# Turning the sorted rows of an MoE stage: blockwise loads and the vector engine in place of TensorE and ACT

## The chip, the cores and the metric

The kernel runs on one core of one Trainium2 chip. The time is the device time of one execution in microseconds (us); lower is better. The engines of a core work side by side, each from its own queue, in order: PE (TensorE: matrix products; its weight loads are listed apart as PEld), DVE (VectorE), ACT (ScalarE), POOL (GpSimd) and SP (SyncE, which here only issues DMAs). Between engines order is kept by semaphores.

## The reference

One transformer block with modulation (adaLN): attention, and behind it a mixture of experts (MoE). The change touches the MoE alone. Cut to that part, it computes:

```python
x = x + ga * attention(h)                       # 2 x 1024 tokens, dim 256, 16 heads
h = _layernorm(x) * (1 + cb) + sb
xf = h.reshape(-1, 256)                         # 2048 tokens
logits = xf @ router_w.T                        # 8 experts
topk_vals, topk_idx = jax.lax.top_k(logits, 2)
topk_w = jax.nn.softmax(topk_vals)
order = jnp.argsort(topk_idx.reshape(-1))       # the 4096 pairs, sorted by expert
x_sorted = xf[order // 2]
y1 = ragged_dot(x_sorted, w1 of each expert)    # 256 -> 2 * 176
gate, up = jnp.split(y1, 2, axis=-1)
y2 = ragged_dot(silu(gate) * up, w2 of each expert)   # 176 -> 256
y = (y2[inv] * topk_w).reshape(T, 2, 256).sum(axis=1)
x = x + gb * y
```

All numbers are float32.

## The kernel before, in words

**Attention, to about 1148 us.** Four blocks of 512 tokens go through 16 heads each. While they run, the tokens of finished blocks are normalised, routed and scattered by POOL's indirect DMAs into `sorted_x`, a DRAM tensor of 39 tiles (`ALL`) of 128 rows in the order of the experts. Each expert's rows are padded to whole tiles. A row has 260 numbers (`ROW`): the token's 256, and four behind them (its weight, its batch, the row of `results` that it goes to). The first 17 tiles (`FULL`) are filled by the first 12 tiles of 128 tokens; the others need the second set of scatters as well, that of the last block's tokens, which runs inside the MoE stage. The weights `w1` (`load_w1`, L355) and `w2` are loaded in the last attention block.

**The MoE stage, from about 1148 us.** Each sorted tile m goes through these steps:

- `Sorted(m)`, L1587: one DMA on SP's queue loads 128 rows of 260 numbers into `x`, one row a partition. It runs up to 7 tiles (`PRE`) ahead, into 2 + 5 buffers of their own and then a ring of 18.
- `turn` (L1594, L1596): the matmul needs the 256 features on the partitions. Two TensorE transposes of 128x128 write `xp` into PSUM, ACT copies it to `xT`.
- `up` (L1603 to L1613): four matmul instructions `su` with the expert's `w1`, ACT's Silu `sg`, DVE's product `sact`.
- `gates` (L1656): DVE makes the output gate of the tile's rows.
- `turn_back` (L1619, L1621): two TensorE transposes `ap`, and ACT's copy `sactT`.
- `down` (L1628 to L1639): four matmul instructions `sy` with `w2`; DVE scales them into `ysb`; POOL scatters the 128 rows to `results` by an indirect DMA.

At the end the rows of `results` are read back (`y`), added in pairs with `xs`, and written out.

The loop over m gives turn of tile m, up of m−1, turn_back of m−3 (m−2 from `LATER` = 24 on) and down of m−4 (m−3 from then on) in one round:

```python
tiles[m].turn()
tiles[m - 1].up()
sooner = m >= LATER
while back < min(m - 2 + sooner, ALL):
    tiles[back].gates()
    tiles[back].turn_back()
    back += 1
while done < min(m - 3 + sooner, ALL):
    tiles[done].down()
    done += 1
```

This order of the source is not quite the order in which an engine meets the instructions: when the program is built, the framework places them in each engine's queue by its own estimate of when their operands are there. On the chip a queue is then fixed, and served in order.

Of the kernel before, what the change touches and what calls it, by code (L numbers as in the profile page):

```python
# [43 lines left out]
FP = mybir.dt.float32  # L44
# [6 lines left out]
P = 128  # L51
# [9 lines left out]
def tile_adaln_attention_moe(  # L61
# [15 lines left out]
    nc = tc.nc  # L77
    B, N, D = x.shape
    DC = D // P
    T = B * N  # L80
    NT = T // P
# [13 lines left out]
    TOP = 2  # L95
    SETS = ((0, (NBLK - 1) * QT), ((NBLK - 1) * QT, NT))


    FULL = -((E * (P - 1) - TOP * SETS[0][1] * P) // P)
# [55 lines left out]
    ident = const.tile([P, P], FP, name="ident")  # L155
# [9 lines left out]
    SIDE = 32  # L165
# [45 lines left out]
    sorted_x = dram.tile([ALL * P, ROW], FP, name="sorted_x")  # L211
    results = dram.tile([(TOP * NT + ALL) * P, D], FP, name="results")

    class Scattered:
# [3 lines left out]
        def __init__(self, name):  # L218
            self.name, self.all = name, []
# [21 lines left out]
    into_x = Scattered("into_x")  # L241
# [5 lines left out]
    with ExitStack() as attn:  # L247
# [100 lines left out]
        w1_at = []  # L348

        def load_w1():  # L350
            w1_in = w1.rearrange("(c p) e i -> p c e i", p=P)
            pieces = []
            for c in range(DC):
                piece = keep.tile([P, E, I2], FP, tag="w1" + "ab"[c], name=f"w1_{c}")
                nc.sync.dma_start(out=piece, in_=w1_in[:, c])  # L355
                pieces.append(piece)
            w1_at.append(pieces)

# [624 lines left out]
        class Settle:  # L983
# [43 lines left out]
            def turn(self, i):  # L1027


                t = self.blk * QT + i  # L1030
                b = t // TPB
                row = rows[:, t, :D]
                mean, rs = self.of_x[i]
                nc.vector.scalar_tensor_tensor(
                    row, xs[:, t, :], mean, one_cb[:, b, :], ALU.subtract, ALU.mult
                )
                nc.vector.scalar_tensor_tensor(row, row, rs, sb[:, b, :], ALU.mult, ALU.add)
                self.rT[i] = self.wide.tile([P, DC, P], FP, tag="h", name=f"rT_{t}")
                if self.blk < NBLK - 1:
                    turned(row, self.rT[i], f"r{t}")  # L1040
                    return
                tp = self.psum.tile([P, DC, P], FP, tag=self.tag, name=f"tp2_{t}")
                for c in range(DC):
                    nc.tensor.transpose(tp[:, c, :], row[:, ts(c, P)], ident)
                nc.scalar.copy(self.rT[i], tp)
# [388 lines left out]
        for blk in range(NBLK):  # L1434
# [11 lines left out]
            for h in range(HEADS):  # L1446
                src = q if h < HEADS - HG else after
# [50 lines left out]
            if blk == NBLK - 1:  # L1498
                at(1, 6, load_wout_again)
                at(11, 0, load_w1)  # L1500
                at(QT + 2, 4, place_first, work)
                slots = [(k, t) for k in range(TOP) for t in range(0, SETS[0][1], 3)]
                for n, (k, t) in enumerate(slots):
                    if k and not t:
                        at(QT + 3 + n, 2, choose_second, *SETS[0])
                    at(QT + 3 + n, 3, on_vector, scatter_some, k, t, 3)
                at(HEADS - HG + 1, 0, load_w2)

            for i, h in enumerate(((6, 8, 11, 13), (7, 9, 11, 13))[blk] if blk < 2 else ()):
                t = TPB + blk * QT + i  # L1510
# [23 lines left out]
    with ExitStack() as moe:  # L1534
# [3 lines left out]
        mg = moe.enter_context(tc.tile_pool(name="mg", bufs=3))  # L1538
# [4 lines left out]
        ps_t = moe.enter_context(tc.tile_pool(name="ps_t", bufs=3, space=PSUM))  # L1543
# [11 lines left out]
        def row_buffer(name):  # L1555


            return mr.tile([P, TOP * D], FP, tag="x", name=name)
# [4 lines left out]
        def expert(m):  # L1563
# [10 lines left out]
                loaded.update(zip(range(m, m1), values))  # L1574
            return loaded[m]

        class Sorted:


            def __init__(self, m):  # L1580
                self.m = m
                if m < EARLY + NEXT:
                    pool = mx if m < EARLY else me
                    self.x = pool.tile([P, ROW], FP, name=f"x_{m}")
                else:
                    self.x = row_buffer(f"x_{m}")[:, :ROW]
                load = nc.sync.dma_start(out=self.x, in_=sorted_x[ts(m, P), :])  # L1587
                into_x.read(load, TOP * (SETS[0][1] if m < FULL else NT))

            def turn(self):  # L1590
                m = self.m
                tp = ps_t.tile([P, DC, P], FP, tag="t", name=f"xp_{m}")
                for c in range(DC):
                    nc.tensor.transpose(tp[:, c, :], self.x[:, ts(c, P)], ident)  # L1594
                self.xT = mg.tile([P, DC, P], FP, tag="xT", name=f"xT_{m}")
                nc.scalar.copy(self.xT, tp)  # L1596

            def up(self):
                m = self.m
# [99 lines left out]
        for m in range(ALL + 3):  # L1699
# [17 lines left out]
            if SCATTERS <= m < SCATTERS + TOP:  # L1717
                k = m - SCATTERS
# [18 lines left out]
        for i in range(BESIDE):  # L1737
            m = ALL - 4 + i // 2
# [59 lines left out]
```

## Time and profile before

| what | value |
|---|---|
| time, median of 3 runs | 1266.76 us (1266.58 to 1268.63) |
| the profiled execution: its time | 1273.54 us |
| the profiled execution: its span, first to last instruction | 1271.8 us |
| granted TensorE clock, mean | 0.995 |
| instructions | 13505 |
| DMA | 79.26 MB in 87975 packets, mean 62 GB/s |

The profile comes from one execution, taken by the hardware profiler. Every engine has a row of busy time; "the chain that ended last" is followed back from the last instruction, at each step to what released it or to the instruction before it on its engine. A group of instructions is given as line, engine, operation, output<-inputs with shapes and count, then its busy time and the mean ns of one, then the idle time of the engine in front of it and what ended that. A span has the length between the first and the last instruction, so it is a little below the time. Matmuls are pipelined and their ends are modelled: where matmuls follow closely, the distance of their starts is the better measure.

The MoE stage takes about 124 of the 1271.8 us. Its 78 xp transposes (L1594) and 39 copies (L1596) are the instructions that the change replaces, for 31 of the 39 tiles.

### The profile page before, as it was taken

To read this page: it belongs to the slowest core of one execution; us is meant where nothing else is said; L and a number is where in the kernel's file an instruction comes from. 1 tells how busy PE (TensorE), PEld (TensorE's weight loads), DVE (VectorE), ACT (ScalarE), POOL (GpSimd) and SP (SyncE) were. 2 spreads that over 40 slices of the span, in tenths; PEclk is the share of its full clock that TensorE was granted. 3 is DMA by queue.
4 is the path that set the end of the run, shared out by engine and by line. 5 is a ranking of instruction groups with operands and counts; after the bars stand their busy time and mean duration, and the time that the engine had idled before them with its cause. 6 is when DMAs were issued, how large, how long until landed. Compare 5 with 4: busy or idle time off the path is not lost.

```text
span 1271.8 us, 13505 instructions
## 1 busy us (share of the span) xinstructions
PE 1244.7 (98%) x4134; PEld 686.0 (54%) x4134; DVE 848.5 (67%) x1763; ACT 452.7 (36%) x884; POOL 187.3 (15%) x223
## 2 busy tenths in 40 slices
PE   8999999999999999999999999999999999999895
PEld 5544444448545454548545454557545444477573
DVE  7577777666866876666866666666758675547355
ACT  3533333331333343431333434321333344314331
POOL 3210301010100201010000000000000223204542
PEclk9999999999999999999999999999999999999998
DMA  7011020211011111111011061012011242113426
GB/s 265 0 34 34 6 83 15 73 35 42 13 44 44 40 48 43 49 38 35 12 51 38 34 198 34 34 54 76 13 56 32 68 141 92 34 34 97 134 84 236
DMA packets 87975, 79.26 MB, mean 62 GB/s; under 512 B 43520, under 2 KB 66688, under 8 KB 87648
## 3 DMA queue, kind: packets, MB, share of 16 engines
q1 hardware_dynamic: 82624, 67.06, 17.3%
q0 software_dynamic: 3408, 9.38, 2.0%
q10 hardware_dynamic: 1872, 1.97, 0.4%
q8 instruction: 34, 0.56, 0.2%
q14 instruction: 37, 0.30, 0.1%
HBM read 58.29 MB, written 20.08 MB: 62 GB/s over the span
## 4 chain that ended last, share of the span: by engine, by line
PE 90%; DVE 3%; POOL 2%; issue 2%; DMA 1%; another core or an unknown queue 0%; ACT 0%; SPq 0%; POOLq 0%; DVEq 0%; ACTq 0%
PE s L767 34%; PE o L782 33%; PE q L693 7%; PE pr L925 6%; PE pr L846 2%; PE su L1603 2%; PE sy L1628 1%; POOL results L1639 1%; PE kv L466 1%; PE q L642 1%; PE ap L1619 0%; PE xp L1594 0%; PE lg L1051 0%; DMA wide_q<-row_q 0%; DVE h L404 0%
## 5 line engine op out<-in xcount | busy, mean ns | idle before, releaser
L767 PE MATMUL s<-qT,kT 128*128 128x512 f32 x1024 | 524.4, 595 | 0.7 <-ACT qT L1310 0.7
L782 PE MATMUL o<-p,vs 128*128 128x512 f32 x1024 | 521.6, 592 | 0.0
L771 ACT ACTIVATE p<-s 128x512 f32<-128x512 f32 x512 | 304.8, 597 | 511.3 <-PE s L767 498.1
L787 DVE TENSOR_TENSOR sum<-sum,p 128x512 f32<-128x512 f32 x384 | 264.2, 688 | 178.8 <-ACT p L771 175.9
L782 PEld LDWEIGHTS o<-p,vs 128*128 128x128 f32 x1024 | 194.3, 190 | 243.5 <-issue 238.7
L767 PEld LDWEIGHTS s<-qT,kT 128*128 128x128 f32 x1024 | 191.5, 190 | 186.4 <-issue 177.2
L742 POOL TENSOR_TENSOR rn_q<-rn_q,minus_half 128x16 f32<-128x16 f32 x15 | 44.1, 2940 | 319.0 <-DVE rn_q L738 300.4
L787 DVE TENSOR_TENSOR sum<-p,p 128x512 f32<-128x512 f32 x64 | 43.9, 685 | 38.5 <-ACT p L771 38.5
L1603 PE MATMUL su<-w,xT 128*128 x156 | 54.2, 471 | 3.6 <-ACT xT L1596 3.5
L551 DVE STREAM_TRANSPOSE turned_q<-sq_q 128x512 f32<-128x512 f32 x60 | 42.4, 707 | 18.2 <-ACT sq_q L655 18.2
L925 PE MATMUL pr<-wout_sb,qT 128*128 128x128 f32 x384 | 50.0, 276 | 0.0
L583 DVE TENSOR_TENSOR qT<-qT,wide_q 128x512 f32<-128x512 f32 x60 | 41.1, 686 | 10.7 <-DMA wide_q<-row_q 10.7
L583 DVE TENSOR_TENSOR qT<-qT,wide 128x512 f32<-128x512 f32 x64 | 43.5, 679 | 6.9 <-DMA wide<-row 6.8
L1639 POOL DMA_INDIRECT results<-ysb,x x39 | 40.4, 1037 | 50.5 <-DVE ysb L1636 39.2
L655 ACT ACTIVATE sq_q<-qT 128x512 f32<-128x512 f32 x56 | 35.2, 629 | 34.6 <-DVE qT L700 26.9
L551 DVE STREAM_TRANSPOSE turned<-sum 128x512 f32<-128x512 f32 x64 | 45.5, 710 | 1.8
L925 PEld LDWEIGHTS pr<-wout_sb,qT 128*128 128x128 f32 x384 | 46.2, 192 | 0.1
L693 PE MATMUL q<-rows,wq_sb 128*128 128x256 f32 x168 | 45.4, 379 | 0.0
L789 ACT COPY qT<-o 128x512 f32<-128x512 f32 x64 | 37.4, 584 | 19.7 <-PE o L782 19.6
L552 DVE TENSOR_REDUCE parts<-turned 128x16 f32<-128x512 f32 x64 | 43.3, 676 | 1.1
L1628 PE MATMUL sy<-w2s,sactT 128*128 x156 | 40.3, 383 | 1.5 <-issue 1.3
L552 DVE TENSOR_REDUCE parts_q<-turned_q 128x16 f32<-128x512 f32 x60 | 40.8, 680 | 0.7
(330 smaller groups left out, 1067.9 us busy)
## 6 DMA issues: line engine op xcount, KB each, us to landing
wide<-row SPq DMA_DIRECT2D x64, 256.0 KB
wide_q<-row_q SPq DMA_DIRECT2D x60, 256.0 KB
sorted_x<-zero SPq DMA_DIRECT2D x1, 5070.0 KB
x<-sorted_x SPq DMA_DIRECT2D x39, 130.0 KB
y<-results SPq DMA_DIRECT2D x14, 256.0 KB
w<-in_w_dram SPq DMA_DIRECT2D x2, 1408.0 KB
wout_sb<-in_wout_dram SPq DMA_DIRECT2D x1, 2048.0 KB
wq_sb<-in_wq_dram SPq DMA_DIRECT2D x1, 1536.0 KB
```

The lines of the kernel that those rows point to most:

```text
L551: nc.vector.transpose(turned.rearrange("p c k -> p (c k)"), src)
L552: latest["vector"] = nc.vector.tensor_reduce(parts[:, i, :], turned, AX.X, ALU.add).ins
L583: nc.vector.tensor_tensor(q.head(h), q.head(h), wide, ALU.mult)
L693: nc.tensor.matmul(ps[:, k, :].rearrange("p (t k) -> p t k", k=P), x, y, start=True, stop=True,)
L767: latest["tensor"] = nc.tensor.matmul(s, kT[:, ts(b * NJ + j, P)], q.head(h), start=True, stop=True).ins
L771: nc.scalar.activation(p, s, AF.Exp)
L782: latest["tensor"] = nc.tensor.matmul(outs[h], vs[:, b * NJ + j, :], p, start=(j == 0), stop=(j == NJ - 1)).ins
L787: latest["vector"] = nc.vector.tensor_tensor(sums[h], first, p, ALU.add).ins
L925: nc.tensor.matmul(ps[:, piece, :], halves(g)[:, pair, head, t, i, :], w[:, g * HG // TWO + pair, :], start=False, stop=(g == NG - 1 and m ...
L1603: nc.tensor.matmul(u, self.xT[:, c, :], w1_flat[c][:, bass.ds(at, I2)], start=(c == 0), stop=(c == DC - 1),)
L1628: nc.tensor.matmul(y, self.actT[:, c, :], w2_flat[:, c * D :][:, bass.ds(at, D)], start=(c == 0), stop=(c == 1),)
L1639: ins = nc.gpsimd.indirect_dma_start(out=results, out_offset=bass.IndirectOffsetOnAxis(ap=self.x[:, TO : TO + 1].bitcast(I32), axis=0), in ...
```

## The change

A tile's features are no longer put on the partitions by TensorE for tiles 8 to 38. DVE has a block transpose: it turns each block of 32 partitions by 32 numbers, but moves no block to other partitions. So the loads move the blocks. A tile's row index is (a, i) with four groups a of 32; its 256 features are split into four groups of 64. Load b of four brings, for all 128 rows, the 64 features of group b, to the 32 partitions of group b, with row group a as the first free index; each run is 256 bytes. Then partition group b holds only features of group b, and DVE's one block transpose of 128 x (4 x 2 x 32) puts feature j of a block on partition j of the group, and the row on the free axis. The fifth load brings the four numbers behind the features.

With that, the feature on partition p = (b, j) of half c is 64 b + 32 c + j, where it was 128 c + p. So `w1` is loaded in the same permuted order, in four pieces of 32 partitions for each half, for all tiles. Tiles 0 to 7 (`FIRST_TILES`) are still turned on TensorE and copied by ACT; their loads permute the features within each row (two DMAs with runs of 128 bytes, and one for the four numbers behind them).

Counted, 62 transposes with their weight loads and 31 ACT copies are gone; 31 DVE transposes of 128x256 are new; SP issues 179 loads of `x` where there were 39, and 8 of `w1` where there were 2.

```diff
         def load_w1():
-            w1_in = w1.rearrange("(c p) e i -> p c e i", p=P)
+            w1_in = w1.rearrange("(b c j) e i -> c b j e i", c=DC, j=SIDE)
             pieces = []
             for c in range(DC):
                 piece = keep.tile([P, E, I2], FP, tag="w1" + "ab"[c], name=f"w1_{c}")
-                nc.sync.dma_start(out=piece, in_=w1_in[:, c])
+                for b in range(P // SIDE):
+                    nc.sync.dma_start(out=piece[ts(b, SIDE)], in_=w1_in[c, b])
                 pieces.append(piece)
...
+        FIRST_TILES = 8
+        in_blocks = sorted_x.rearrange("(m a i) d -> m i a d", a=P // SIDE, i=SIDE)
+
         class Sorted:
...
-                load = nc.sync.dma_start(out=self.x, in_=sorted_x[ts(m, P), :])
-                into_x.read(load, TOP * (SETS[0][1] if m < FULL else NT))
+                n = D // (P // SIDE)
+                parts = [(self.x[:, D:], sorted_x[ts(m, P), D:])]
+                if m < FIRST_TILES:
+                    src = sorted_x[ts(m, P), :D].rearrange("p (b c j) -> c p b j", c=DC, j=SIDE)
+                    for c in range(DC):
+                        parts.append((self.x[:, ts(c, P)].rearrange("p (b j) -> p b j", j=SIDE), src[c]))
+                else:
+                    for b in range(P // SIDE):
+                        to = self.x[ts(b, SIDE), :D].rearrange("i (a k) -> i a k", k=n)
+                        parts.append((to, in_blocks[m][:, :, ts(b, n)]))
+                for to, src in parts:
+                    with nc.allow_non_contiguous_dma(reason="some numbers of each row"):
+                        load = nc.sync.dma_start(out=to, in_=src)
+                    into_x.read(load, TOP * (SETS[0][1] if m < FULL else NT))
 
             def turn(self):
-                m = self.m
-                tp = ps_t.tile([P, DC, P], FP, tag="t", name=f"xp_{m}")
-                for c in range(DC):
-                    nc.tensor.transpose(tp[:, c, :], self.x[:, ts(c, P)], ident)
-                self.xT = mg.tile([P, DC, P], FP, tag="xT", name=f"xT_{m}")
-                nc.scalar.copy(self.xT, tp)
+                self.xT = mg.tile([P, DC, P], FP, tag="xT", name=f"xT_{self.m}")
+                if self.m < FIRST_TILES:
+                    tp = ps_t.tile([P, DC, P], FP, tag="t", name=f"xp_{self.m}")
+                    for c in range(DC):
+                        nc.tensor.transpose(tp[:, c, :], self.x[:, ts(c, P)], ident)
+                    nc.scalar.copy(self.xT, tp)
+                    return
+                nc.vector.transpose(
+                    self.xT.rearrange("p c (a i) -> p a c i", i=SIDE),
+                    self.x[:, :D].rearrange("p (a c j) -> p a c j", c=DC, j=SIDE),
+                )
```

## The prediction

> **What bounds the kernel now.** I read the page first: busy shares, clock row, and the shares of the chain that ended last.
>
> ```profile
> PE 1244.7 (98%) x4134; PEld 686.0 (54%) x4134; DVE 848.5 (67%) x1763; ACT 452.7 (36%) x884; POOL 187.3 (15%) x223
> ...
> PEclk9999999999999999999999999999999999999998
> ...
> PE 90%; DVE 3%; POOL 2%; issue 2%; DMA 1%; another core or an unknown queue 0%; ACT 0%; SPq 0%; POOLq 0%; DVEq 0%; ACTq 0%
> ```
>
> TensorE is the bound over the whole program, at full clock. But the change lives in the last tenth, the stage of the 39 sorted tiles, so next I read the chain in order of time there.
>
> ```profile
> 1203.96 1.19 PE su L1603 x4
> 1205.36 0.86 PE sy L1628 x4
> 1206.45 1.19 PE su L1603 x4
> ```
>
> One tile lasts 1206.45 − 1203.96 = 2.49 us (2.488 by the raw starts): su 1.19, two ap transposes 0.22, sy 0.87, and two xp transposes 0.22 in the hole ahead of the next su. PE has no gap. It has none because it works on four tiles at once: between su of tile k and su of tile k+1 it does ap of k−2, sy of k−3 and xp of k+2, so every result has a tile's time or more to come back through ACT and DVE. The groups of the stage give the costs:
>
> ```profile
> L1594 PE MATMUL xp<-ident,x 128*128 128x128 f32 x78 | 15.0, 274 | 0.3 <-ACT proj L869 0.3
> L1596 ACT COPY xT<-xp 128x256 f32<-128x256 f32 x39 | 14.6, 375 | 31.2 <-PE xp L1594 24.7 <-remote 3.8 <-PE su L1603 1.9
> L1636 DVE SCALAR_TENSOR_TENSOR ysb<-sy,x,gate 128x256 f32<-128x256 f32 x32 | 15.4, 482 | 14.6 <-PE sy L1628 9.2 <-remote 3.6 <-PE xp L1594 1.5
> ```
>
> ACT and DVE idle in front of these because they wait for PE. Last, the timeline of the last tile, where nothing is left to overlap with it. It is the one place in this profile that shows what a tile costs alone:
>
> ```profile
> 1251.94 1.35 PE L1603 MATMUL su<-w,xT 128*128 x4
> ...
> 1253.32 0.32 ACT L1611 ACTIVATE sg<-su 128x176 f32<-128x176 f32 x1 [1.62 <-PE su L1603]
> ...
> 1253.67 0.34 DVE L1613 TENSOR_TENSOR sact<-sg,su 128x176 f32<-128x176 f32 x1
> ...
> 1254.06 0.29 PEld L1619 LDWEIGHTS ap<-ident,sact 128*128 128x128 f32 x2
> ...
> 1254.68 0.37 ACT L1621 COPY sactT<-ap 128x256 f32<-128x256 f32 x1 [0.71 <-PE ap L1619]
> ...
> 1255.31 0.73 PEld L1628 LDWEIGHTS sy<-w2s,sactT 128*128 128x128 f32 x4 [0.27 <-ACT sactT L1621]
> ```
>
> From the first su matmul to the first possible ap transpose pass 1254.20 − 1251.94 = 2.27 us; from that transpose to sactT's end 1255.05 − 1254.20 = 0.85 us.
>
> **The change part by part.** The basis is the profiled execution: span 1271.8, time 1273.54. It is 6.8 us above the median of 1266.76. Three tiles from 1178.7 to 1193.8 take 15.1 us instead of 7.5 there (first stretch under the rivals), about that difference. I apply differences to the median.
>
> *Removed from PE.* 31 tiles × 2 transposes. The group's 274 ns is a modelled length: the two start 0.109 us apart and move su by 0.217 us. Where PE is the bound, that is 0.217 us a tile, 31 × 0.217 = 6.7 us at most. The Trainium skill (VectorE: DVE Perf Modes, The three transpose paths) prices a TensorE transpose of 128x128 at 390 ns, which would make it 62 × 0.39 = 24 us. The raw starts decide: 6.7.
>
> *Removed from ACT.* 31 copies of 0.375: off the path, since ACT waits for PE.
>
> *Added to DVE.* 31 block transposes of 128x256. The nearest row has the same shape:
>
> ```profile
> L437 DVE STREAM_TRANSPOSE blocks_r<-rows 128x256 f32<-128x256 f32 x12 | 5.3, 441 | 0.0
> ```
>
> I take 0.44. DVE has 0.48 + 0.34 + 0.48 = 1.30 us a tile; 1.74 is under any period below. Price on the path 0, and 0.44 a tile if DVE were late.
>
> *Loads.* Tiles 0 to 7 take 3 DMAs instead of 1, tiles 8 to 38 take 5, all on SP's queue: 179 issues instead of 39. Back to back the old loads are issued 0.474 us apart, and landed in 2.1 to 3.1 us, with eight in flight at most. Five cost 2.37 us a tile. Tiles 8 to 16 have all their issues by 1148 + (18 + 45) × 0.474 = 1178, ahead of their use. Tiles 17 and later may only start after the second set of scatters, at 1186.2: 22 × 2.37 = 52 us, until 1238, some 2.4 us a tile. Tile 2 lands about 0.5 us late at the start (three issues from 1148.1 and a landing of 2.5 make 1151.6; its xp ran at 1151.27). I charge 0.5. How the 256-byte runs that change partitions issue and land is not shown. The nearest row is a load of 32 partitions in 128-byte runs (ns shortest, median, longest):
>
> ```profile
> L455 SPq DMA_DIRECT2D rT<-turned_r x96: 302/430/792, 342.0 to 957.3; - x96
> ```
>
> Its median is that of the x loads back to back (0.43), it landed in 1.5 to 1.8 us, its longest is 0.79. So the bounds are 0.474 an issue and 0.84 (0.79 and the 0.045 between two), 2.4 to 4.2 us a tile. I take 0.474, by the median.
>
> *w1.* 8 DMAs instead of 2 between 1037 and 1058 us, some ninety us ahead of use, beside attention's matmuls: 0. Without that cover, 6 × 0.47 = 2.8 us.
>
> *Moved: the order on PE.* This decides. Nothing in the source reorders up, turn_back and down, but the order of an engine's queue is fixed when the program is built, by the framework's own estimate of when operands will be there, and the changed program has another. Listed by tile:
>
> ```
> before  xp[k+1] su[k] ap[k-2] sy[k-3]                          (1 tile later from 35 on)
> after   su[13] ap[11] sy[10] | su[15] ap[14] sy[13] ap[15] sy[14]
>         su[17] sy[16] ap[17] | su[18] sy[17] ap[18] | su[19] sy[18] ap[19]
>         su[20] sy[19] ap[20] sy[20] | su[21] sy[20] ap[21] sy[21]
>         su[22] ap[22] sy[22] | su[23] ap[23] sy[23] | ... | su[38] ap[38] sy[38]
> ```
>
> From tile 22 on, PE does a whole tile before it starts the next: seventeen times what the old program does once, at its end. ap[k] waits at the head of PE's queue for DVE's sact[k], and behind it su[k+1], whose xT is long there, waits too. The Trainium skill (TensorE: Matmul & The Clock Gate, Part 2, Step-by-step) says that matmuls stay in program order, and only weight loads are pulled ahead. The trace has no matmul overtaking another. If they could overtake, the 6.7 us would stand; as they can't, each tile costs its latency.
>
> Period of a serial tile: 2.27 (su to ap) + 0.85 (ap, copy) + 0.05 (wait to weight load) + 0.97 (0.10 from sy's weight load to its matmul, 0.87 for sy until the next su starts) = 4.13 us. Taken with the lag that the last sy showed behind its predecessor (0.27 instead of 0.05) it is 4.35.
>
> - Tiles 8 to about 14: 9 × 0.217 = −1.95 (xp of 8 to 16); but by tile 15 PE has done one ap and sy pair (0.22 + 0.87) more: −0.9.
> - su[15] to su[22]: now 1211.26 − 1193.84 = 17.4. Afterwards 3.4 for tile 15; 2.5 for each of 16 to 19, because ap[k] follows 2.27 us behind su[k] with 0.22 of its own; 3.7 and 4.1 for 20 and 21: 21.1, +3.7.
> - su[22] to su[38]: now 1251.94 − 1211.26 = 40.7. Afterwards 16 × 4.13 = 66.1: +25.4 (by 4.35: +28.9).
> - The end: tile 38 takes as long as now, but the two earlier tiles' scatters no longer queue on POOL ahead of its own (issued at 1255.48, 1256.74, 1258.01; alone it could go at about 1256.7): −1.3.
> - The start: +0.5.
>
> Sum: −0.9 + 3.7 + 25.4 − 1.3 + 0.5 = +27.4. So 1266.8 + 27.4 = 1294 us; a profiled execution like the one shown would be 1301.
>
> The loads are hidden here: with 4.13 us a tile SP's 2.4 is no bound. POOL (1.08 a scatter) and ACT (0.69 a tile) are not either.
>
> **The rivals.**
>
> *Faster.* PE stays packed and each of 31 tiles saves 0.217: 1266.8 − 6.7 = 1260. For it: PE is the bound, DVE has room. Against it: it needs PE to start su[k+1] while ap[k] waits. To break even, the serial tiles would have to run in 4.13 − 27.4/16 = 2.4 us, but su to ap alone is 2.27 of that. Chance 0.04.
>
> *The loads bound it.* If an issue or landing is above 0.83 us (4.13 / 5), SP is slower than the serial chain: at 1.0 us an issue tiles 17 to 38 take 22 × 5 = 110, load 38 is issued at 1186 + 110 = 1296 in the trace's time and lands at 1298.5, against su[38] at 1251.9 + 28.7 = 1281 there: 18 more, 1312. For it: short runs, partition changed; eight in flight with 4 us landings would do half of that. Against it: the median of the row above, and DMA engines that are busy 0.32 of the stretch from 1211 to 1252 (shown next). Chance 0.05. Were the PE order the old one, the loads at 0.474 would give 2.37 to 2.42 a tile, 1265 to 1269: no change; 0.02.
>
> *The clock falls.* In the serial tiles PE works 2.27 of 4.13 us, in bursts with gaps up to about 1.1 us. Stretches of the stage, with busy time and instructions of PE, its weight loads, DVE, ACT and POOL, then clock, DMA share and GB/s:
>
> ```profile
> 1178.70:1193.84 15.14, 10.15 (x38) 6.63 (x37) 4.09 (x11) 3.36 (x11) 8.87 (x9) 0.89 0.55 174
> 1193.84:1211.26 17.42, 17.42 (x86) 13.04 (x85) 9.15 (x22) 7.14 (x21) 7.56 (x7) 1.00 0.38 106
> 1211.26:1251.94 40.68, 40.68 (x199) 30.63 (x198) 19.72 (x47) 16.59 (x49) 17.53 (x17) 1.00 0.32 106
> 1251.94:1261.00 9.06, 4.51 (x21) 3.11 (x19) 6.62 (x20) 1.02 (x3) 3.96 (x5) 1.00 0.90 330
> ```
>
> In the first, PE idled 2.8 us and the clock then was 0.5 for 3.4 us, an su taking 2.71 instead of 1.19; in the last, with PE busy half the time, it stayed 1.00. The skill's rule (TensorE: Matmul & The Clock Gate, The two states) puts a cold clock behind an idle window of about 3.4 us, which these gaps don't fill. At half clock PE's 2.27 doubles: up to 6.4 a tile, +36 more, 1330. In part of the stage only: 1305 to 1315. Chance 0.08.
>
> *Not what it says.* That the transposes don't go can be left out: the instructions of the changed program are 16 xp and 8 copies, for tiles 0 to 7.
>
> **How the numbers follow.** Serial tiles 0.81: 1294, by itself 1287 to 1302 (period 3.9 to 4.35 gives −4 to +4, the loads' start and the stretch around tile 15 ±3). Clock 0.08, loads 0.05, no change 0.02, faster 0.04. For the range I take in the lower end of the serial case and the near parts of the clock and load cases: 1285 to 1305. 0.2% is 2.5 us, about what a measurement of this kernel can tell from no change. Faster 0.04, same 0.02, slower 0.94.
>
> **What would show it.** In the trace after, su starts 4.1 us apart from tile 22 on; in its groups, ap idle behind DVE sact, about 1 us a tile, and sy behind ACT sactT, about 0.7; xp in 16 matmuls and copies xT 8; a DVE transpose at 0.44 x31; clock row unchanged; PE's share down to about 97%. Wrong, if su starts come 2.3 to 2.5 apart in the last 16 tiles (order not binding), if the idle ahead of xT or su is released by the DMA x<-sorted_x (loads bound), or if su takes 2.7 us there (clock).

## The result, and the profile after

The changed kernel takes 1303.69 us in the median (1303.14 to 1305.73), the kernel before 1266.74 on the same chip: a ratio of 1.0292 (95% interval 1.0279 to 1.0305), 37.0 us slower. The profiled execution has a span of 1303.9 us and a time of 1305.73, 2.0 us above its median; that of before lay 6.8 us above its own. The page, busy shares, clock and shares of the last chain:

```profile
PE 1249.2 (96%) x4072; PEld 678.4 (52%) x4072; DVE 857.5 (66%) x1794; ACT 441.9 (34%) x853; POOL 184.7 (14%) x223
...
PEclk9999999999999999999999999999999999999997
...
PE 85%; issue 5%; DVE 3%; POOL 3%; DMA 2%; SPq 1%; POOLq 0%; ACT 0%; DVEq 0%; ACTq 0%
```

PE still has most of the chain, but "issue" (time in which an engine waited for nothing that the profile shows) and POOL have come in: in the serial tiles the chain is followed from one scatter of POOL's to the next, through gaps. So the cost is read from PE's waits below, not from these shares. The groups of the stage show that the edit is what it says: 16 transposes and 8 copies are left, 31 DVE transposes are there, each at 438 ns.

```profile
L1619 DVE STREAM_TRANSPOSE xT<-x 128x256 f32<-128x256 f32 x31 | 13.6, 438 | 0.0
...
L1616 PE MATMUL xp<-ident,x 128*128 128x128 f32 x16 | 3.4, 283 | 0.3 <-ACT proj L872 0.3
L1617 ACT COPY xT<-xp 128x256 f32<-128x256 f32 x8 | 3.0, 377 | 4.0 <-PE xp L1616 4.0
```

Now the stage cut at the starts of su[0], su[13], su[17], su[22], su[38] (busy time and instructions of PE, its weight loads, DVE, ACT, POOL; then clock, DMA share, GB/s):

```profile
1149.99:1180.02 30.03, 29.75 (x141) 22.01 (x142) 24.38 (x105) 11.84 (x34) 13.89 (x17) 1.00 0.56 108
1180.02:1197.85 17.83, 13.78 (x54) 8.87 (x52) 8.59 (x21) 3.31 (x10) 12.09 (x14) 0.90 0.43 119
1197.85:1216.45 18.60, 14.57 (x55) 8.97 (x56) 8.40 (x22) 3.45 (x10) 6.01 (x7) 1.00 0.47 99
1216.45:1282.98 66.53, 44.84 (x161) 25.89 (x160) 21.87 (x56) 11.02 (x32) 15.34 (x16) 1.00 0.37 104
1282.98:1303.90 20.92, 2.92 (x11) 1.45 (x9) 12.92 (x36) 0.69 (x2) 2.03 (x3) 0.62 0.48 163
```

The fourth row is the largest part of the loss: 16 tiles in 66.5 us (4.16 each), with PE busy 44.8 of them, DVE 21.9, ACT 11.0. No engine is full. What PE waited for in that stretch (us in total, times, longest):

```profile
PE ap L1645 <- DVE sact L1639: 12.5, 16, 0.8
PE sy L1654 <- ACT sactT L1647: 8.3, 16, 0.5
PE su L1629 <- PE sy L1654: 1.0, 3, 0.3
```

Each of the 16 tiles waits once for sact and once for sactT; the three entries of su hold no wait for xT or a load. One of them (tile 35) in the timeline:

```profile
1270.76 1.35 PE L1629 MATMUL su<-w,xT 128*128 x4
...
1272.14 0.32 ACT L1637 ACTIVATE sg<-su 128x176 f32<-128x176 f32 x1 [2.40 <-PE su L1629]
1272.49 0.34 DVE L1639 TENSOR_TENSOR sact<-sg,su 128x176 f32<-128x176 f32 x1 [1.05 <-ACT sg L1637]
1272.74 0.44 DVE L1619 STREAM_TRANSPOSE xT<-x 128x256 f32<-128x256 f32 x1
...
1272.88 0.44 PE L1645 MATMUL ap<-ident,sact 128*128 128x128 f32 x2 [0.78 <-DVE sact L1639]
1273.41 0.37 ACT L1647 COPY sactT<-ap 128x256 f32<-128x256 f32 x1 [0.95 <-PE ap L1645]
...
1273.83 1.13 PE L1654 MATMUL sy<-w2s,sactT 128*128 x4 [0.52 <-ACT sactT L1647]
...
1274.80 0.75 PE L1629 MATMUL su<-w,xT 128*128 x2
```

This is the chain that the timeline of before showed once, for its last tile, now once per tile: 1274.80 − 1270.76 = 4.04 us. The same cut for both, by the starts of su in the two traces (us):

| profiled execution | start of su[0] | su[0] to [12] | [12] to [17] | [17] to [22] | [22] to [38] | su[38] to the end |
|---|---|---|---|---|---|---|
| before | 1149.62 | 29.08 | 20.12 | 12.44 | 40.68 | 19.86 |
| after | 1149.99 | 27.76 | 20.10 | 18.60 | 66.54 | 20.92 |
| difference | +0.37 | −1.32 | 0.0 | +6.2 | +25.9 | +1.1 |

They sum to the 32.1 us between the spans. In both of these executions tiles 12 to 16 contain a slow stretch (at 2.49 a tile they would take 12.4 us, here 20.1). The profile of before is 6.8 us longer than its median, about what that stretch adds (7.7); the changed kernel's is only 2.0 longer. The difference of the two, 4.8 us, is what is left between 32.1 and 37.0. That the slow stretch is what lengthens the profile of before is argued: no shorter execution of it was profiled.

### The profile page after: what moved, and what is told of

The parts are those of the page before. It is cut to its first block, busy times and chain, and to the rows that moved or that the text cites. A ratio compares the mean times of both kernels' runs of the same rounds, so it can differ in the third digit from the quotient of the medians.

```text
span 1303.9 us, 13516 instructions
## 1 busy us (share of the span) xinstructions
PE 1249.2 (96%) x4072; PEld 678.4 (52%) x4072; DVE 857.5 (66%) x1794; ACT 441.9 (34%) x853; POOL 184.7 (14%) x223
## 4 chain that ended last, share of the span: by engine, by line
PE 85%; issue 5%; DVE 3%; POOL 3%; DMA 2%; SPq 1%; POOLq 0%; ACT 0%; DVEq 0%; ACTq 0%
PE s L770 33%; PE o L785 33%; PE q L696 7%; PE pr L928 6%; PE pr L849 2%; POOL results L1665 2%; SPq L1608 1%; PE su L1629 1%; PE kv L469 1%; PE sy L1654 1%; PE q L645 1%; PE lg L1054 0%; DMA wide_q<-row_q 0%; DVE h L407 0%; DMA y<-results 0%
## 5 line engine op out<-in xcount | busy, mean ns | idle before, releaser
L792 ACT COPY qT<-o 128x512 f32<-128x512 f32 x64 | 37.3, 582 | 19.8 <-PE o L785 19.6
```

## The experiments

The runs were made on several chips. On some the kernel before took 1267 us, on others 1274 to 1275 (about what its profiled execution took), so a kernel is compared here with the runs of before on its own chip, and across chips only by the spacing of su.

"Held" below means: from m = 14 of the main loop on, the named queue's instructions of the sorted tiles stand in the order of the source. It adds no wait and no work of its own, but the framework then places the other queues anew, so the order of those has to be read as well:

```diff
+        def hold(ins):
+            engine = ins.ins.engine
+            if held[0] and engine in last_on:
+                tc.add_manual_dep(ins.ins, last_on[engine].ins.name,
+                    mybir.DependencyInfo(mybir.DependencyClass.NoSync, mybir.DependencyReason.DATA),
+                    reason="in this order")
+            last_on[engine] = ins
+            return ins
...
-                    nc.tensor.matmul(
+                    hold(nc.tensor.matmul(
```

**old_loads_serial: the serial order with the old loads and transposes.** The kernel before, with PE's queue held and the lags set to none from m = 23 on (`turn` moves behind `up` there as well):

```diff
+            serial = m >= 23
...
-            while back < min(m - 2 + sooner, ALL):
+            while back < min(m if serial else m - 2 + sooner, ALL):
...
-            while done < min(m - 3 + sooner, ALL):
+            while done < min(m if serial else m - 3 + sooner, ALL):
```

> The kernel before, with its one load a tile and its transposes on PE and ACT; only PE's queue is held from tile 22 on in the serial order su[k] xp[k+2 or so] ap[k] sy[k]. Order theory: su starts 4.05 to 4.2 us apart for 16 tiles instead of 2.5, xp in the gap behind su at no price: about +26 us, 1290 to 1296 us. Loads theory: the loads are those of before, so no more than a few us, 1267 to 1272 us.

Measured: 1300.76 us against 1274.39, ratio 1.0198 (1.0181 to 1.0215): +26.4 us. From su[23] on the starts are 4.05 to 4.42 us apart (4.42 again at su[24], [28] and [32]), and the waits are those of the changed kernel:

```profile
PE sy L1643 <- ACT sactT L1636: 10.5, 16, 2.7
PE ap L1634 <- DVE sact L1628: 8.0, 14, 0.8
```

With the loads and transposes of before, the serial order costs 26 us. It is sufficient for the 25.9 us between su[22] and su[38]. Its sorted tiles have no DVE transpose and no permuted load.

**three_loads: the loads alone.** `FIRST_TILES = ALL`, so that no tile is turned on DVE.

> The changed kernel with all 39 tiles in the form of its first eight: three permuted loads a tile with 128-byte runs, transposes on PE and copies on ACT, no DVE transpose; w1 in eight loads. PE's order comes out as before the change. Order theory: as before but for 0.4 us at the start, 1266 to 1268.5 us. Loads theory (contention of many short runs): three fifths of the issues and more and shorter packets, some 10 us and more over the kernel before.

Measured: 1273.71 against 1274.39, ratio 0.9997 (0.9985 to 1.0009); su[22] to su[38] in 40.68 us, exactly as before. Three loads a tile with 128-byte runs, and `w1` in eight, cost nothing that this comparison can tell. It does not test the five loads of a tile; two_queues and both_held do.

**order_held: PE's order undone.** The changed kernel with PE's queue held.

> The changed kernel with all its loads and DVE transposes; only PE's queue is held, from tile 13 on, in the order of the source (su[k] ap[k-2] sy[k-3], and su[k] ap[k-1] sy[k-2] from tile 23 on). Order theory (PE's serial order is the price): the serial stage goes, su starts 2.27 to 2.45 us apart, so 31 x 0.217 = 6.7 us are gained less 0.4 at the start: 1260 to 1264 us. Loads theory (five DMAs a tile on SP, or their contention, set the pace, and the order only follows them): su stays 3 us and more apart in tiles 17 to 38, 1290 to 1304 us.

Measured: 1304.09 against 1274.39, ratio 1.0232 (1.0214 to 1.025). Nothing regained: a clear miss of the order theory as I had it, and the time and the spacing of su fall where the loads theory had put them. But it was not the loads either: in the tile shown, the transpose has no wait in front of it at all. PE's wait, and a tile of that trace:

```profile
PE su L1644 <- DVE xT L1634: 30.2, 23, 4.2
```

```profile
1258.89 1.42 PE L1644 MATMUL su<-w,xT 128*128 x4 [1.02 <-DVE xT L1634]
...
1260.35 0.32 ACT L1652 ACTIVATE sg<-su 128x176 f32<-128x176 f32 x1 [2.88 <-PE su L1644]
1260.37 1.03 PE L1669 MATMUL sy<-w2s,sactT 128*128 x4
...
1260.70 0.34 DVE L1654 TENSOR_TENSOR sact<-sg,su 128x176 f32<-128x176 f32 x1 [1.95 <-ACT sg L1652]
1261.44 0.48 DVE L1677 SCALAR_TENSOR_TENSOR ysb<-sy,x,gate 128x256 f32<-128x256 f32 x1 [0.40 <-PE sy L1669]
1261.84 0.44 DVE L1634 STREAM_TRANSPOSE xT<-x 128x256 f32<-128x256 f32 x1
```

DVE's queue closes a loop of its own. The transpose of tile k+1 stands behind sact[k] and ysb[k−2]; ysb waits for the sy that PE does after su[k]; and su[k+1] waits for the transpose. That is 3.53 us a tile, in places 4.05. Before the change no step between x and su was on DVE. This order on DVE is not the one that the changed kernel has in its serial tiles: there the queue goes sact[k], xT[k+1], ysb[k] by the starts in the trace, and no su waits for xT; with PE held it goes sact[k], ysb[k−2], xT[k+1]. So in tiles 22 to 38 of the changed kernel PE's order is the lock; DVE's lock is met there in tiles 17 to 19 (below), and over the whole stage once PE's is opened.

**both_held and dve_held.** The four DVE steps of a tile (transpose, sact, gate, ysb) are held as well, so that xT[k+1] comes ahead of sact[k]; or DVE alone is held.

> The changed kernel, with PE's and also DVE's queue held in the order of the source from tile 13 on: on DVE xT[k+1] now stands ahead of sact[k]. Two-orders theory (with PE held, DVE still turned tile k+1 behind sact[k] and an ysb, and that loop took 3.5 to 4.05 us): su starts 2.27 to 2.45 us apart from tile 17 on, by PE or by SP's five issues (2.37); less what the stretch of tiles 12 to 16 may lose, a ratio to the kernel before of 0.993 to 1.001. Loads theory (xT is late because x is): su starts still 3.4 us and more apart, ratio 1.015 to 1.025.

> As both_held with DVE's queue held alone; PE then gets the order su[k+1] ap[k] sy[k] su[k+2] from tile 24 on. Two-orders theory: what is between two su then is the wait for sactT, not the whole chain: 1.19 + 0.22 + 0.85 + 0.05 + 0.87 = about 3.1 us a tile for 14 tiles instead of 2.49, +8.5, less about 3 gained in the other tiles: ratio 1.003 to 1.008. Theory that any of the two queues held is enough: 2.27 to 2.45 us a tile, ratio 0.993 to 0.998. Loads theory: no better than the change, 1.02 and more.

Measured, on one chip: both_held 1270.81 against 1267.46, ratio 1.0025 (1.0015 to 1.0036); dve_held 1279.42, ratio 1.0093 (1.0077 to 1.0108). So with both queues held 3.4 us are left of the 37, and with DVE's alone 12. But dve_held is not the changed kernel with its PE order kept: the framework placed PE's queue anew, su[k+1] ap[k] sy[k] in place of su[k] ap[k] sy[k]. From tile 25 on su is 3.05 to 3.53 us apart (expected 3.1), and its only frequent wait is the one named:

```profile
PE sy L1671 <- ACT sactT L1664: 7.2, 14, 0.5
```

The ratio of dve_held came out a little above what was expected, and so did that of both_held. Where both_held lost its gain, its trace shows in three places. First DVE waits for the rows of tile 17, which need the last block's scatters and then five issues:

```profile
1192.48 0.45 DVE L1636 STREAM_TRANSPOSE xT<-x 128x256 f32<-128x256 f32 x1 [4.00 <-DMA x<-sorted_x]
```

Then, from tile 22 on, DVE waits for the rows of 12 of the 16 tiles, and the last chain runs through SP's issues and a load for one tile after another (start, us, what):

```profile
DVE xT L1636 <- DMA x<-sorted_x: 12.5, 12, 2.0
```

```profile
1222.27 0.43 SPq L1625
1222.74 2.30 DMA x<-sorted_x
```

Su[22] to su[38] took 39.56 us there, 2.47 a tile; where PE sets the pace it takes 37.36 (below). Third, the end is longer: 23.5 us from su[38] on, against 19.8 in the profile of before. SP's last load of x was issued only 3.7 us ahead of su[38], where it was 32 us ahead. Behind it on the same queue, the first fetches of y began 1.9 us ahead of su[38] instead of 6.4, and the last four were issued 12.7 to 13.5 us behind it instead of 9.8 to 10.4.

**both_ahead: the transpose one tile earlier still.** In the loop, `turn` of tile m+1 is called in place of that of m.

> As both_held, with each DVE transpose one tile earlier in the source, so that xT[k+2] stands ahead of sact[k]. Two-orders theory: no more to gain where PE is the bound already, su 2.27 us apart; what it may gain is in the stretch of tiles 12 to 17, where DVE waits for free ysb buffers: as both_held or up to 3 us less, ratio 0.992 to 0.998. Loads theory: no gain over both_held, since xT can't start before x has landed.

Measured: 1269.98, ratio 1.0022 (1.0013 to 1.0031): with both_held's within the interval, and outside of what was expected for it. It cannot pass the landing of the rows either: from 1200 us on DVE waits 16 times for them, 19.6 us in all.

**two_queues: the framework chooses again.** Two of a tile's five loads go to ACT's queue; nothing is held.

> The changed kernel with two of the five loads of each tile issued by ACT instead of SP; nothing is held. The framework then gives PE the old order (su[k] ap[k-2] sy[k-3]). Order theory: the serial stage goes, but ACT's queue now waits for the second set of scatters in front of ten issues around tile 17 (about 4 us), so 1260 to 1268 us. Loads theory: with 3 x 0.474 us a tile on SP the loads are faster too, so it also gets faster; this run alone tells the two apart only together with the first.

Measured: 1275.9 against 1274.39, ratio 1.0012 (1.0002 to 1.0021). From tile 16 on su is 2.27 us apart (su[22] to su[38]: 37.36 us, against 40.68 before), with five loads and DVE's transposes, so neither of these costs 37 us. The gain was lost in two places. At tiles 3 and 4, ACT issued four loads from 1156.01 on and came to sactT only at 1158.75; su[0] to su[12] took 32.39 us instead of 27.76. That was not expected. At tile 15 more was lost than the 4 us that I had put on it, su[16] coming 12.46 us behind su[15]: ACT's Silu stood behind ten load issues that waited for the scatters.

```profile
1191.81 5.87 ACTq L1609 DMA_DIRECT2D x<-sorted_x  x10
1197.78 0.32 ACT L1638 ACTIVATE sg<-su 128x176 f32<-128x176 f32 x1 [10.48 <-DMA x<-sorted_x]
```

**mid_only.** DVE for tiles 8 to 16 alone, three loads and PE for the others.

> The changed kernel with the DVE transpose for tiles 8 to 16 alone (the tiles whose rows are there early); tiles 17 to 38 go in the form of the first eight, with three loads, PE and ACT. Nothing is held; PE's order is the old one but for one tile. Two-orders theory: 9 x 0.217 = 2 us gained less 0.4 at the start, if the stretch of tiles 12 to 16 doesn't eat them: ratio 0.998 to 1.001.

Measured: 1270.18 against 1267.46, ratio 1.0019 (1.001 to 1.0028), slower than expected. Su[0] to su[12] shrank by 1.3 us, as in every kernel with this edit whose loads are all on SP, and su[22] to su[38] was 40.68 as before. So about 4 us are lost between su[12] and su[22], an estimate from the two medians. The trace shows a wait of that size (the profiled execution is 3.8 us above the median): an ysb stood 4.14 us for a buffer, and behind it in DVE's queue the transpose that su[16] needed, which began at 1194.25, as in the changed kernel (below).

```profile
1192.16 0.48 DVE L1662 SCALAR_TENSOR_TENSOR ysb<-sy,x,gate 128x256 f32<-128x256 f32 x1 [4.14 <-DMA results<-ysb,x]
```

In both_held and dve_held on the same chip, where xT stands further ahead in DVE's queue, su[12] to su[17] took 15.64 and 14.48 us instead of 18.70.

**four_loads and pe_at_seams: fewer issues.** From both_held, the tails (the four numbers) are loaded in two DMAs for all of DVE's tiles:

```diff
-                parts = [(self.x[:, D:], sorted_x[ts(m, P), D:])]
...
+                    if m in (FIRST_TILES, FULL):
+                        m1 = FULL if m < FULL else ALL
+                        group = me.tile([P, m1 - m, ROW - D], FP, name=f"tails_{m}")
+                        tails.append((m, group))
+                        parts.append((group, sorted_x[m * P : m1 * P, D:].rearrange("(t p) k -> p t k", p=P)))
```

In pe_at_seams, also (feature 2p + c on partition p of half c, so DVE reads with a stride of two, and a tile that PE turns comes in one load):

```diff
-            w1_in = w1.rearrange("(b c j) e i -> c b j e i", c=DC, j=SIDE)
+            w1_in = w1.rearrange("(p c) e i -> p c e i", c=DC)
...
+        def on_pe(m):
+            return m < FIRST_TILES or m in (17, 18)
```

> both_held with one thing changed: the four numbers behind the features are no longer loaded tile by tile, but by one DMA for tiles 8 to 16 and one for tiles 17 to 38, so a tile of DVE's takes four issues on SP instead of five (1.90 us instead of 2.37). Theory that SP's issues are what both_held ends on (its tiles 17 to 38 came 2.40 us apart on the average, and the fetches of y stood behind the loads): su 2.27 us apart except where the source changes its lag, the wait at tiles 17 and 18 about 2.5 us shorter, y fetched earlier: 4 to 6 us under both_held, ratio to the kernel before 0.9975 to 0.999. Rival (DVE's queue or the end of the kernel holds both_held, not SP): no more than 1 us under both_held, ratio 1.001 to 1.003.

> four_loads, with the features split into halves by stride two (feature 2p + c on partition p of half c) instead of in blocks of 32. So w1 takes two loads again, and a tile that PE turns takes one load, with a strided weight load; tiles 0 to 7 do that, and also 17 and 18, the first two behind the second scatters. DVE reads its blocks with stride two. Expected by the theory: the wait for the rows of 17 (four issues, 1.9 us, become one) shrinks by 1.4 us and the first tiles lose nothing; 2 x 0.217 us are given back: 0.5 to 1.5 us under four_loads, ratio 0.996 to 0.9985. Rival: a stride of two costs DVE or PE's weight load so much that nothing is left: equal to four_loads or above.

Measured, on one chip (before: 1274.75): four_loads 1271.8, ratio 0.9976 (0.9966 to 0.9986); pe_at_seams 1271.32, ratio 0.997 (0.9959 to 0.9981). Su[22] to su[38] takes 37.36 us in both; the half microsecond between the two is within the noise. These beat the kernel before on that chip, by 3 us. On a chip where the kernel before takes 1267 us neither was run, so it is not shown that they would beat it there. Since both_held had been run on another chip, it was run again beside pe_at_seams:

> both_held again, beside pe_at_seams on one chip, since the two were measured on different chips, on which the kernel before stood at 1267.5 and at 1274.8 us. Theory (SP's issues hold both_held): its tiles 17 to 38 take 52 to 53 us, and it is 4 to 7 us above pe_at_seams. Rival (the two chips made the difference): the two are within 2 us.

> pe_at_seams again, on the same chip as both_held: 4 to 7 us under it, tiles 17 to 38 in 48.7 us. Against the kernel before: 0.996 to 0.998 if that has its slow stretch around tile 13 on this chip, 0.999 to 1.002 if it has not.

Measured (before: 1274.99): both_held 1272.91, ratio 0.9988 (0.9979 to 0.9997); pe_at_seams 1271.54, ratio 0.9975 (0.9963 to 0.9988). The rival was right: only 1.4 us lie between them. Here both_held had the slow stretch (su[12] to su[17] in 21.34 us instead of 15.64), in which SP got ahead with its loads: those of tile 22 were issued 8.0 us ahead of su[22], in the first both_held 4.6. Su[22] to su[38] then took 37.36 us with five issues as well. In these two profiles SP's five issues bind only where the slow stretch does not give them time. What four issues are worth without the slow stretch was not run.

## Why the prediction was right, point by point

- *The order on PE decides.* Right, and shown alone by old_loads_serial (+26.4 us). su[22] to su[38] was put at 66.1 us and measured 66.5. That this is so close is in part luck: the period was put at 4.13 and is 4.05 in most tiles (the waits for sact and sactT are 0.78 and 0.52 us instead of about 1 and 0.7), and every fourth tile takes about 4.5 for a reason that the prediction did not have (below); the mean is 4.16.
- *What it left out: DVE's order.* The step that it put at nothing was the DVE transpose: "Price on the path 0, and 0.44 a tile if DVE were late". Its 0.44 us was right, and the check made was of DVE's busy time (1.74 us a tile against the period); its place in the queue was not looked at. In the stretch su[15] to su[22] I had put 2.5 us for each of the tiles 16 to 19, from ap and su alone. Tiles 17 to 19 took 3.24 to 3.44:

```profile
1202.37 1.03 PE L1654 MATMUL sy<-w2s,sactT 128*128 x4
...
1203.44 0.48 DVE L1662 SCALAR_TENSOR_TENSOR ysb<-sy,x,gate 128x256 f32<-128x256 f32 x1 [0.18 <-PE sy L1654]
1203.84 0.43 DVE L1619 STREAM_TRANSPOSE xT<-x 128x256 f32<-128x256 f32 x1
...
1204.42 0.53 PE L1629 MATMUL su<-w,xT 128*128 x1 [0.67 <-DVE xT L1619]
```

  sy, ysb, xT, su in turn: the lock that order_held later showed by itself. Tiles 17 to 21 took 18.6 us; my periods make 15.3 of them, 3.3 too few. Over all of su[12] to su[22], with the slow stretch of both profiles inside, +3.7 was put and +6.1 came.
- *Around tile 15* the same queue bound a scatter to the next su: an ysb waited 4.00 us for a buffer whose scatter was still on its way, and the transpose that su[16] needed stood behind it.

```profile
1190.32 0.48 DVE L1662 SCALAR_TENSOR_TENSOR ysb<-sy,x,gate 128x256 f32<-128x256 f32 x1 [4.00 <-DMA results<-ysb,x]
...
1192.43 0.44 DVE L1619 STREAM_TRANSPOSE xT<-x 128x256 f32<-128x256 f32 x1
```

  In the profile of before this stretch is as long, but otherwise: ACT and DVE both stand there, and the profile names nothing of this program that they wait for.

```profile
1189.10 0.48 DVE L1636 SCALAR_TENSOR_TENSOR ysb<-sy,x,gate 128x256 f32<-128x256 f32 x1 [3.59 <-remote]
1189.20 0.37 ACT L1596 COPY xT<-xp 128x256 f32<-128x256 f32 x1 [3.79 <-remote]
```

  So the two profiles do not show it as a loss. Between the medians some 4.8 us are left (37.0 − 32.1), and this is the likely place: mid_only, in which PE and DVE have the same order up to su[15] and no tile is serial, lost about 4 us between su[12] and su[22] against a kernel before that took 1267 us. An execution of before without its slow stretch was not profiled, so it is argued and not shown.
- *PE's transposes at 0.217 us a tile* instead of 0.78 by the price of 390 ns (which is for bf16; these numbers are float32): right. From tile 6 to 12 su comes 2.27 us apart instead of 2.49.
- *The loads:* 0.43 us an issue, 0.474 from one to the next, landing in 2.0 us in the median (1.7 to 3.4), where the row of `rT` had 1.5 to 1.8. Hidden in the changed kernel, as said; not in both_held, where they became the bound that the rival described, at 2.4 us a tile.
- *The clock* stayed at 1.00 from su[17] to su[38], PE being busy two thirds of the time in the serial tiles, in gaps of 0.3 to 0.8 us. That rival fell. But the 3.4 us of idle that the prediction puts ahead of a cold clock were more than these traces needed: behind 2.74 us of idle PE (until 1191.65) the clock was 0.50 from 1192.38 to 1195.80, as it was behind 2.82 us before the change; 2.50 us in both_ahead left it at 1.00. Here the measurement decides. (The 2.71 us of four su at half clock belong beside 1.35 in the same view at full clock, not beside the 1.19 that the prediction gives.)
- *The end* was put at −1.3 and is +1.1. The last scatter did come earlier, 5.0 us behind su[38] instead of 6.1. But the last fetches of y were issued at 1293.45 to 1295.15, up to 12.2 us behind su[38]; before it was 9.8 to 10.4. On ACT's queue they now stand behind six writes of the output, and SP, which before waited for the scatters alone, waited for such a write as well:

```profile
SPq L1690 <- DMA out_dram<-y: 2.6, 1, 2.6
```

  The queues of the end had not been compared.

Together, from the +27.4: start and first tiles 0.6 lower (−1.0 where −0.4 was put), su[12] to su[22] 2.4 higher, the serial tiles 0.5 higher, the end 2.4 higher, and the medians add 4.8: +37. The sign, the mechanism and the largest term stood. The size did not: 1303.7 us is 9.7 above the 1294, above the 1287 to 1302 that the prediction gives the serial case by itself, and inside 1285 to 1305 only through the room left for the clock and the loads, neither of which came. In that the range was lucky.

## What to carry to other kernels

Moving one step to another engine also moves where it stands in that engine's queue, and a framework that orders queues by estimates may reorder the others with it: read the order on every engine that the step's operands pass through, not only on the bound one, and ask of each instruction what stands ahead of it that belongs to the tile before. A software pipeline can be locked in two queues, and opening one of them may then show no gain (order_held), which must not be read as proof against the first; nor does a gain from opening one (dve_held) tell which lock it was, if the other queue was placed anew with it. Freeing 0.22 us of the bounding engine is worth little if the data come at a fixed time or the transfers' issues need longer than what is left of the period.

## What the runs showed of the hardware that was not expected

Every fourth serial tile took about 0.47 us more (4.52 instead of 4.05 at su[24], [28], [32]). There PE's own queue reads four experts' numbers into registers (`expert`, AT_ONCE = 4): the trace has it at 1227.76 with 998 ns, and the weight load of the next su, which otherwise starts while sy's loads are running, starts after it, at 1229.04. The serial tiles of old_loads_serial have the same at the same tiles (4.42 instead of 4.05). In the packed order of before the period stays at 2.49 us over the same reads. No run moves the reads, so the cause is read from the order of the trace and not tested.

A DVE transpose that reads with a stride of two (pe_at_seams) took 434 ns in the median, with blocks of 32 in both_held_pair 435, and left the tile at 2.27 us. A PE weight load with a stride of two took 198 ns instead of 142; tile 4, which PE turns, took 2.50 us instead of 2.49.

The slow stretch around tile 13 comes and goes. Su[12] to su[17] took 20.1 us in the profile of before, where 2.49 a tile makes 12.4. With both queues held it took 14.0 and 15.6 us on the chip where before takes 1267, and 21.3 to 23.3 on the two chips where before takes 1275. Its cause stays open.
